# Second image of the first pair in chunks of 484 pixels, from rings of slots, in a polynomial convolution and attention kernel

## The chip, the cores and the metric

The kernel runs on one core of one Trainium2 chip. The metric is the device time of one execution in microseconds (us). A core has five engines with an instruction queue each: TensorE (PE, matmuls into PSUM), VectorE (DVE), ScalarE (ACT), GpSimd (POOL) and SyncE (SP). Transfers (DMAs) between HBM and SBUF are issued by instructions in the queues of SP and ACT. Instructions of one queue run in order; engines wait for each other through semaphores.

## The reference

The input x is 32 images of 64 channels and 56 x 56 = 3136 pixels, in float32. Two layers follow each other.

```
# layer 0, per group of 8 channels (8 groups), per pixel
p2 = x[:, :, _I2] * x[:, :, _J2]                 # 36 products of two
y2 = einsum('bgihw,goi->bgohw', p2, W2) + b2
p3 = x[:, :, _I3] * x[:, :, _J3] * x[:, :, _K3]  # 120 products of three
y3 = einsum('bgihw,goi->bgohw', p3, W3) + b3
l = inp + y2 * beta2 + y3 * beta3 * CONV3_SCALE
# layer 1, per image
g = clip(bn(conv1x1(l, w_inside)), 0, 6)
theta = l[:, :32]
f = einsum('niab,nicd->nabcd', theta, theta)     # 3136 x 3136 scores
f = softmax(f over the first pixel index)
f = softmax(f over the second pixel index)
out = einsum('nabcd,nicd->niab', f, g) / h * w
out = bn(depthwise_conv3x3(out)) + l
```

The scores are symmetric, so the first softmax of a column is that of a row, and both are done on a tile of 128 rows and 3136 columns.

## The kernel before, in words

The 32 images are worked on as 16 pairs (n = 0 to 15). The two images of a pair share the 128 partitions. Per pair there are IT = 49 tiles of attention: 24 of 128 pixels for each image and one that holds the last 64 pixels of both.

A tile t runs as follows. `scores` (twice, the two halves of the 3136 columns) multiplies theta by theta on PE into PSUM tile ps, and DVE turns the sign and keeps the minimum (tile e, first and second half; nm is the running minimum). `first_softmax` and `second_softmax` are two exponentials on ACT over 128 x 3136. Three tiles later `attend` multiplies e by g on PE into the accumulators av and the front of ax. So a tile has two half-steps, each with a `scores`, half an `attend`, and one place ("aux0", "aux1") for a unit of other work on PE.

The units are the polynomial of layer 0 and the 1x1 convolution g, both into the back of the same PSUM bank, ax. The polynomial of an image pair is cut in chunks of PCH = 242 pixels (NPC = 13, list PCS, line 37). Per chunk and per k (k counts the four groups of 32 partitions of outputs; ALL is the four of a pair, TWO the two of the second image alone) five rotated copies of x are loaded (names 0, a, 2, 4, b; b comes as two DMAs of 64 partitions), and for the whole chunk one pair c. POOL multiplies: q = x0 * xa, then four products p of q with 0, 2, 4 and b, and one product of the pair c. PE then multiplies six rounds (q, four p, the c product) by weights into ax (`poly`, line 452), and DVE adds bias and x and writes y (`poly_out`, line 469). A unit of the first pair's second image has three rounds, a unit of a whole pair two.

The order of all queues is written out in Python: `Pinned` (line 100) chains the instructions of an engine in the order of the calls. The loop at line 889 goes tile by tile. It calls `advance`, which drives the generators `products` (POOL's multiplications) and `prefetch`, which starts loads in the order of `plan` while there is room (`held` against `XB`, line 315: 7 slots for x0, 13 for the other copies, 3 for c) and credit (up to 8 transfers for a half-step in the first pair). `ROOM` (line 359) is the same for products: 8 slots for q, 20 for the others.

The first image of pair 0 goes another way (lines 222 to 297 and 747 to 797): seven chunks of FW = 448 pixels, loads in turn by SP's and ACT's queues (`first_loads`), products on DVE (`first_products`), polynomial into PSUM banks of their own (`first_poly`), output by DVE (`first_out`), then g (`first_g`). The batch norms of layer 1 (lines 285 to 302) stand after the products of chunk 1 and before the output of chunk 0; they need two square roots on ACT (`rsqrt_eps`). At chunk 5 `load_theta` starts for the first 2240 pixels, and the loads of the second image are fed with a credit of 12. After the last output `load_theta` loads the other 896 pixels, as four DMAs on SP's queue.

The second image of pair 0 (TWO, 13 chunks, 26 units) and the whole of pair 1 (ALL, 13 chunks, 39 units), with nine g units each, are then spread over the 98 half-steps of pair 0. Later pairs have one pair's units in theirs.

What the change touches: the batch norms, `load_next` (326), `prefetch` (354), `products` (362), `poly` (452), `poly_out` (469), `load_theta` (483), `poly_unit` (720), the loop at 780 and `rounds` (809).

Of the kernel before, what the change touches and what calls it, by code (L numbers as in the profile page):

```python
# [9 lines left out]
FP = mybir.dt.float32  # L10
AF = mybir.ActivationFunctionType
ALU = mybir.AluOpType
# [4 lines left out]
C = G * CPG  # L17
CRED = C // 2
H = W = 56
N = H * W  # L20
# [13 lines left out]
AUX = (NBL - NK * PER) * CG  # L34
NPC = -(-N // (BANK - AUX))
PCH = -(-N // NPC)
PCS = [(p, min(PCH, N - p)) for p in range(0, N, PCH)]
NROT = 6
EXT = CPG + NROT - 1
GM = 3  # L40
# [16 lines left out]
NRND = 5  # L57
# [12 lines left out]
def tile_poly_conv_attention(  # L70
# [61 lines left out]
    at = 0  # L132
# [40 lines left out]
    def col(name):  # L173
        return colt[:, COLS.index(name) : COLS.index(name) + 1]

    def row(name):
        return rowt[:, ROWS.index(name), :]
# [27 lines left out]
        return [t[:, p : p + FW] for t in tiles for p, _ in FCS]  # L205

    fx, fp = parts(firsts), parts(ys[1:] + [tt])
    fat = {"x": 0, "p": 0, "q": 0}
    fxs = {}
    frs = {}  # L210

# [70 lines left out]
    first_loads(2)  # L282


    s1 = rsqrt_eps("bn1", row("var1"), C)
    dve.tensor_tensor(s1, s1, row("gamma1"), ALU.mult)
    for j in range(2):
        dve.tensor_tensor(wit[:, j, :], wit[:, j, :], s1, ALU.mult)
    bias1 = const.tile([128, C], FP, name="bias1")
    dve.tensor_tensor(bias1, row("mean1"), s1, ALU.mult)  # L290
    dve.tensor_tensor(bias1, row("beta1"), bias1, ALU.subtract)
    bias1r = const.tile([128, GM, C], FP, name="bias1r")
    for k in range(GM):
        dve.tensor_copy(bias1r[:, k, :], bias1)


    s2 = rsqrt_eps("bn2", col("var2"), 1)
    dve.tensor_tensor(s2, s2, col("gamma2"), ALU.mult)
    dve.tensor_scalar(wdt, wdt, s2, W / H, ALU.mult, ALU.mult)
    bias2 = const.tile([128, 1], FP, name="bias2")  # L300
    dve.tensor_tensor(bias2, col("mean2"), s2, ALU.mult)
    dve.tensor_tensor(bias2, col("beta2"), bias2, ALU.subtract)

    prods = {}
    NB = 5
    BLK = [(b * H // NB, (b + 1) * H // NB) for b in range(NB)]
# [2 lines left out]

    XB = {"x0": 7, "xs": 13, "xc": 3}
    held = dict.fromkeys(XB, 0)
    plan = []
    loaded = {}
    PACE = 4.5
    credit = [1e9]  # L320

    def start(out, in_):
        credit[0] -= 1
        sync.dma_start(out=out, in_=in_)

    def load_next():
        tag, key = plan.pop(0)
        n, c, ks, name, k = key
        p0, w = PCS[c]
        held[tag] += 1  # L330
        ident = f"{n}_{c}_{ks[0]}_{k}"
        if name == "c":
            t = xp.tile([128, 2, PCH], FP, name=f"xc_{ident}", tag=tag, bufs=XB[tag])
            at = slice(ks[0] * 32, ks[-1] * 32 + 32)
            for d in range(2):
                src = bass.AP(
                    x.tensor,
                    ((4 * n + ks[0]) * EXT + 4 * d) * 4 * N + p0,
                    [[EXT * 4 * N, len(ks)], [N, 32], [1, w]],
                )  # L340
                start(t[at, d, :w], src)
            loaded[key] = [t[at, d, :w] for d in range(2)]
            return
        t = xp.tile([128, PCH], FP, name=f"x{name}_{ident}", tag=tag, bufs=XB[tag])
        for s0, every, d, grow in LOADS[name]:
            src = bass.AP(
                x.tensor,
                ((4 * n + k) * EXT + d) * 4 * N + p0,
                [[N, 32], [grow * 4 * N, NSLOT // every], [1, w]],
            )  # L350
            start(t[s0::every, :w] if every > 1 else t[:, :w], src)
        loaded[key] = t[:, :w]

    def prefetch():
        while plan and held[plan[0][0]] < XB[plan[0][0]] and credit[0] >= 1:
            load_next()


    ROOM = {"q": 8, "pr": 20}
    taken = dict.fromkeys(ROOM, 0)  # L360

    def products(n, c, ks):

        p0, w = PCS[c]
        ident = f"{n}_{c}_{ks[0]}"

        def use(name, k=None):  # L370
            key = n, c, ks, name, k
            return loaded.pop(key)

        x0 = {}
        rounds = [{}]
        both = []
        prods[n, c, ks] = rounds, both
        yield "q", len(ks)
        for k in ks:
            yield "load", (n, c, ks, "a", k)  # L380
            x0[k] = use("0", k)
            xa = use("a", k)
            q = prp.tile([128, PCH], FP, name=f"q_{ident}_{k}", tag="q", bufs=ROOM["q"])[:, :w]
            pool.tensor_tensor(q, x0[k], xa, ALU.mult)
            rounds[0][k] = q
            held["xs"] -= 1
            prefetch()
        for r, of in enumerate(("0", "2", "4", "b")):
            rounds.append({})
            yield "pr", len(ks)  # L390
            for k in ks:
                if of != "0":
                    yield "load", (n, c, ks, of, k)
                xr = x0[k] if of == "0" else use(of, k)
                p = prp.tile([128, PCH], FP, name=f"p_{ident}_{k}_{r}", tag="pr", bufs=ROOM["pr"])[:, :w]
                pool.tensor_tensor(p, rounds[0][k], xr, ALU.mult)
                rounds[-1][k] = p
                held["x0" if of == "0" else "xs"] -= 1
                prefetch()
        at = slice(ks[0] * 32, ks[-1] * 32 + 32)  # L400
        yield "load", (n, c, ks, "c", None)
        yield "pr", 1
        both += use("c")
        p4 = prp.tile([128, PCH], FP, name=f"p4_{ident}", tag="pr", bufs=ROOM["pr"])[at, :w]
        pool.tensor_tensor(p4, both[0], both[1], ALU.mult)
        rounds.append({k: p4 for k in ks})

# [41 lines left out]
                ax[:, AUX : AUX + GM * C].rearrange("p (q c) -> p q c", c=C), bias1r  # L449
            )  # L450

    def poly(n, c, ks, rs):

        p0, w = PCS[c]
        rounds = prods[n, c, ks][0]
        at = slice(ks[0] * 32, ks[-1] * 32 + 32)
        for r in rs:
            for k in ks:
                pe.matmul(
                    out=ax[k * 32 : k * 32 + 32, AUX : AUX + w],  # L460
                    lhsT=wq[:, r, k % 2, :] if r < NRND else w4[at, k * 32 : k * 32 + 32],
                    rhs=rounds[r][k],
                    start=False,
                    stop=(r == NRND),
                    skip_group_check=True,
                )
            taken["pr" if r else "q"] -= 1 if r == NRND else len(ks)

    def poly_out(n, c, ks):

        p0, w = PCS[c]
        at = slice(ks[0] * 32, ks[-1] * 32 + 32)
        assert n < 3 or all((n - 3, b) in stored for b in range(NB))
        xc = prods.pop((n, c, ks))[1][0]
        held["xc"] -= 1
        dve.scalar_tensor_tensor(
            ys[n % 3][at, p0 : p0 + w], ax[at, AUX : AUX + w], bias0[at], xc, ALU.add, ALU.add
        )


    ths = {}

    def load_theta(b, c0=0, c1=N):
        y = ys[b // 2 % 3]
        p0 = (b % 2) * C
        if c0 == 0:
            ths[b] = thp.tile([128, N], FP, name=f"th_{b}", tag=f"th{b % 2}")
        for r in range(4):
            start(ths[b][r * 32 : r * 32 + 32, c0:c1], y[p0 : p0 + CRED, c0:c1])

    def g_in(n, qs, j):

# [191 lines left out]
            f()  # L684

    LAG = 3
    ALL, ONE, TWO = (0, 1, 2, 3), (0, 1), (2, 3)
    last = NP * IT


# [26 lines left out]

            put(hs // 2, f"aux{hs % 2}", go)

    def poly_unit(n, c, ks, rs, hs):  # L720
        ends = rs[-1] == NRND
        unit(
            hs,
            FOR_POLY,
            lambda: poly(n, c, ks, rs),
            (lambda: poly_out(n, c, ks)) if ends else None,
            1 + 3.6 * len(rs),
        )
        if ends and c == NPC - 1:
            for j in (0, 1):  # L730
                if 2 * j in ks:

                    t = hs // 2 + 1 if j == 0 or n == 0 else (n * IT) + 2
                    put(t, "loads", lambda j=j: load_theta(2 * n + j))
# [39 lines left out]
                g_out(0, qs, 0)  # L774
                prepare(FOR_G if qs[0] < NQ else FOR_POLY)

    prepare(FOR_G)
    NF = len(FCS)
    first_poly(0)
    for c in range(1, NF):  # L780
        first_poly(c)
        first_out(c - 1)
        if c + 2 < NF:
            first_loads(c + 2)
        if c + 1 < NF:
            first_products(c + 1)
        if c == 5:
            load_theta(0, 0, FCS[5][0])

            for b in range(NPC):  # L790
                feed(0, b, TWO)
            credit[0] = 12
            advance()
        first_g(c - 1)
    first_out(NF - 1)
    load_theta(0, FCS[5][0], N)
    first_g(NF - 1)


# [4 lines left out]
    for n in range(NP):  # L804
# [2 lines left out]
        ga = [("g", n + 1, qs, 0) for qs in GS]  # L807

        def rounds(m, c, ks, per):
            return [("p", m, c, ks, list(range(r, r + per))) for r in range(0, NRND + 1, per)]  # L810

        todo = []
        if n == 0:
            for c in range(NPC):
                todo += rounds(0, c, TWO, 3)
            todo += gb
            for c in range(NPC):
# [188 lines left out]
```

## Time and profile before

| what | value |
|---|---|
| median of 3 runs | 4962.83 us (4959.59 to 4973.32) |
| the profiled execution, its own time | 4963.24 us |
| span of the profiled execution | 4961.4 us |
| busy share PE, ACT, DVE, POOL | 95%, 92%, 83%, 65% |
| mean granted TensorE clock | 0.988 |
| chain that ended last, by engine | PE 76%, DVE 12%, DMA 3%, issue 3%, ACT 3%, POOL 1%, SPq 1% |

How to read it. A busy row has the busy time of an engine, its share of the span and the instructions. In the slices each digit is tenths of a slice of 124 us. All recorded instructions carry line 108 (the helper), so groups are told apart by tiles: `first` and `first_s` are buffers of the first image, x, xa, xb and xc the loads of later chunks, q and p their products, ps the scores, e the softmax tile, th theta. A row of the timeline has start, length, engine, operation, output and inputs with shape, how many follow each other, and in brackets the idle time before it with what ended it. SPq and ACTq are DMA issues of SP's and ACT's queue.

### The profile page before, as it was taken

The page shows a single profiled execution, that of the slowest core. Times are in us where ns is not written, and L with a number is a line of the kernel's source. Part 1 is how long each engine was busy: PE and PEld are TensorE (multiplying, and loading weights), DVE is VectorE, ACT ScalarE, POOL GpSimd, SP SyncE. Part 2 cuts the span into 40 slices and gives each one's busy share as a digit, 9 for nine tenths or more (in the row PEclk, how much of TensorE's full clock was granted, in tenths as well). Part 3 has the DMA queues.
Part 4 walks back from the last instruction along what each step waited for, and adds up shares of the span by engine and source line. Part 5 has one row for each costly group of instructions (what it writes and reads, how often), then busy time and mean ns, then how long its engine had stood idle before and what let it go on. Part 6 is the DMA issues. An engine that isn't in the chain of part 4 may idle for free.

```text
span 4961.4 us, 263901 instructions
## 1 busy us (share of the span) xinstructions
PE 4711.5 (95%) x118068; PEld 3211.9 (65%) x118068; DVE 4136.2 (83%) x6106; ACT 4554.6 (92%) x2356; POOL 3212.2 (65%) x4325
## 2 busy tenths in 40 slices
PE   6988999999999999999999999999999999999885
PEld 2555666666666666666666666666666666666663
DVE  6545898988888898898988888888888888888787
ACT  1767999999999999999999999999999999999995
POOL 2676685857758586785857678585876858587000
PEclk9999999999999999999999999999999999999997
DMA  7555656565565556556565555656555565654101
GB/s 203 148 154 150 147 143 154 144 149 143 146 148 147 139 150 149 139 143 150 146 146 148 147 142 144 145 152 145 144 150 144 145 145 146 153 142 117 39 8 33
DMA packets 884029, 685.64 MB, mean 138 GB/s; under 512 B 290892, under 2 KB 868428, under 8 KB 878796
## 3 DMA queue, kind: packets, MB, share of 16 engines
q1 hardware_dynamic: 874892, 659.46, 52.1%
q8 instruction: 923, 15.12, 1.3%
q10 hardware_dynamic: 8000, 9.30, 0.6%
q14 instruction: 214, 1.75, 0.1%
HBM read 565.65 MB, written 25.69 MB: 119 GB/s over the span
## 4 chain that ended last, share of the span: by engine, by line
PE 76%; DVE 12%; DMA 3%; issue 3%; ACT 3%; POOL 1%; SPq 1%; ACTq 0%; POOLq 0%; DVEq 0%
PE av L108 33%; PE ps L108 25%; PE ax L108 18%; DVE e L108 10%; ACT e L108 3%; DMA xc_None<-in_x_dram 2%; DVE y L108 1%; SPq L108 1%; POOL p L108 1%; DVE num L108 1%; DMA x<-in_x_dram 1%; DMA first<-in_x_dram 1%; POOL q L108 0%; DMA xa<-in_x_dram 0%; ACTq L108 0%
## 5 line engine op out<-in xcount | busy, mean ns | idle before, releaser
L108 PEld LDWEIGHTS av<-gq,e 128*64 128x64 f32 x64512 | 2015.8, 138 | 945.6 <-issue 938.6
L108 ACT ACTIVATE e<-e,nm 128x3136 f32<-128x3136 f32 x784 | 2283.6, 2913 | 279.9 <-DVE e L108 264.0
L108 POOL TENSOR_TENSOR p<-q,x 128x242 f32<-128x242 f32 (+1 forms) x2418 | 1820.2, 786 | 842.6 <-PE ax L108 834.8
L108 ACT ACTIVATE e<-e,rz 128x3136 f32<-128x3136 f32 x784 | 2270.5, 2896 | 0.0
L108 PE MATMUL av<-gq,e 128*64 128x65 f32 x64512 | 2229.3, 225 | 4.3 <-ACT e L108 3.0
L108 DVE TENSOR_SCALAR_CACHE_REDUCE e<-ps 128x1568 f32<-128x1568 f32 x784 | 1403.4, 1790 | 312.7 <-PE ps L108 295.4
L108 DVE TENSOR_SCALAR_CACHE_REDUCE e<-ps,nm 128x1568 f32<-128x1568 f32 x784 | 1448.3, 1847 | 256.9 <-PE ps L108 251.4
L108 PE MATMUL ps<-th 32*64 32x392 f32 x25088 | 1450.2, 515 | 120.6 <-DVE e L108 110.8
L108 DVE SCALAR_TENSOR_TENSOR y<-tt,wdt,y 128x605 f32<-128x605 f32 (+4 forms) x720 | 726.2, 1009 | 6.7 <-DMA tt<-tr 5.2
L108 POOL TENSOR_TENSOR p<-q,xb 128x242 f32<-128x242 f32 x806 | 574.9, 740 | 218.8 <-PE ax L108 208.5
L108 POOL TENSOR_TENSOR q<-x,xa 128x242 f32<-128x242 f32 x806 | 570.9, 732 | 204.9 <-DMA xa<-in_x_dram 195.5
L108 PEld LDWEIGHTS ps<-th 32*64 32x64 f32 x25088 | 369.9, 130 | 463.1 <-DVE e L108 381.6
L108 PE MATMUL ax<-gq,e 128*64 128x65 f32 x12288 | 490.3, 222 | 1.2 <-issue 1.2
L108 PE MATMUL ax<-p,wq 128*32 128x242 f32 (+1 forms) x6448 | 477.8, 374 | 2.4 <-POOL p L108 1.4
L108 PEld LDWEIGHTS ax<-gq,e 128*64 128x64 f32 x12288 | 425.4, 138 | 1.5 <-issue 1.5
L108 PEld LDWEIGHTS ax<-p,wq 128*32 128x32 f32 x6448 | 178.4, 109 | 108.4 <-POOL p L108 15.7
L108 POOL TENSOR_SCALAR y<-y,bias 128x616 f32<-128x616 f32 (+1 forms) x80 | 149.1, 1864 | 149.2 <-PE ax L108 149.2
L108 DVE SCALAR_TENSOR_TENSOR y<-ax,bias,xc_None 128x242 f32<-128x242 f32 (+3 forms) x208 | 97.1, 467 | 120.7 <-PE ax L108 115.1
L108 POOL TENSOR_TENSOR p<-xc_None 128x242 f32<-128x242 f32 (+3 forms) x208 | 127.6, 614 | 105.2 <-DMA xc_None<-in_x_dram 85.3
L108 PE MATMUL ax<-p,w 128*32 128x242 f32 (+1 forms) x1612 | 125.1, 373 | 33.2 <-POOL p L108 33.2
L108 PE MATMUL ax<-wit,y 128*64 128x64 f32 x3136 | 143.8, 223 | 10.2 <-issue 6.1
L108 ACT ACTIVATION_READ_ACCUMULATOR e<-e,nm 128x1 f32 x784 | 145.7, 186 | 0.0
(80 smaller groups left out, 1348.9 us busy)
## 6 DMA issues: line engine op xcount, KB each, us to landing
x<-in_x_dram SPq DMA_DIRECT2D x2232, 121.0 KB
xa<-in_x_dram SPq DMA_DIRECT2D x744, 121.0 KB
xb<-in_x_dram SPq DMA_DIRECT2D x1488, 60.5 KB
th<-y SPq DMA_DIRECT2D x124, 392.0 KB
xc_None<-in_x_dram SPq DMA_DIRECT2D x360, 121.0 KB
x<-in_x_dram SPq DMA_DIRECT2D x186, 116.0 KB
out_dram<-y SPq DMA_DIRECT2D x64, 308.0 KB
tt<-tr SPq DMA_DIRECT2D x128, 100.0 KB
```

What stands on the lines that cost most here:

```text
L108: i = f(*args, **kw)
```

## The change

Chunks of the second image of pair 0 become 484 pixels wide for loads and for products (six of 484 and one of 232); matmuls and outputs stay at 242 wide, as two parts (sub) of a chunk, each with its two units. Where the slots for x0, the other copies, c, q and the products were buffers of a pool, each kind is now one tile used as a ring; a wide load or product takes two neighbouring slots. The rings for loads have 6 and 14 slots. The c pair of a wide chunk takes the whole c ring. Room is given back when the last part of a chunk has been used.

The batch norms move into the loop, after the products of chunk 2. The loop calls the g of chunk 5 after the output of chunk 6 and after the second part of theta, which goes by ACT's queue.

```diff
+DCS = [(p, min(2 * PCH, N - p)) for p in range(0, N, 2 * PCH)]
...
-    XB = {"x0": 7, "xs": 13, "xc": 3}
+    XB = {"x0": 6, "xs": 14, "xc": 3}
...
-    def start(out, in_):
+    def start(out, in_, queue=sync):
         credit[0] -= 1
-        sync.dma_start(out=out, in_=in_)
+        queue.dma_start(out=out, in_=in_)
+
+    ring = {t: [xp.tile([128, m, PCH], FP, name=f"ring_{t}", tag=t, bufs=1), 0] for t, m in XB.items() if t != "xc"}
+    ringc = xp.tile([128, 2 * XB["xc"] * PCH], FP, name="ring_xc", tag="xc", bufs=1)
+
+    def chunks(ks):
+        return DCS if len(ks) < len(ALL) else PCS
+
+    def many(w):
+        return -(-w // PCH)
+
+    def take_ring(tag, w):
+        t, at = ring[tag]
+        m, size = many(w), t.shape[1]
+        if at % m or at + m > size:
+            at = 0
+        ring[tag][1] = (at + m) % size
+        return t[:, at : at + m, :].rearrange("p m w -> p (m w)")[:, :w]
...
-        held[tag] += 1
+        held[tag] += XB["xc"] if name == "c" and many(w) > 1 else many(w)
...
     def prefetch():
-        while plan and held[plan[0][0]] < XB[plan[0][0]] and credit[0] >= 1:
+        while plan and credit[0] >= 1:
+            tag, (_, c, ks, _, _) = plan[0]
+            m = many(chunks(ks)[c][1])
+            if held[tag] + (XB[tag] if tag == "xc" and m > 1 else m) > XB[tag]:
+                return
             load_next()
...
-                    rhs=rounds[r][k],
+                    rhs=rounds[r][k][:, px],
...
-            taken["pr" if r else "q"] -= 1 if r == NRND else len(ks)
+            if ends:
+                taken["pr" if r else "q"] -= (sub + 1) * (1 if r == NRND else len(ks))
...
-        xc = prods.pop((n, c, ks))[1][0]
-        held["xc"] -= 1
+        xc = prods[n, c, ks][1][0][:, px]
+        if ends:
+            del prods[n, c, ks]
+            held["xc"] -= XB["xc"] if sub else 1
...
-    prepare(FOR_G)
     NF = len(FCS)
     first_poly(0)
     for c in range(1, NF):
...
         if c + 1 < NF:
             first_products(c + 1)
+        if c == 1:
+
+            s1 = rsqrt_eps("bn1", row("var1"), C)
...
+            prepare(FOR_G)
         if c == 5:
             load_theta(0, 0, FCS[5][0])
 
-            for b in range(NPC):
+            for b in range(len(DCS)):
                 feed(0, b, TWO)
             credit[0] = 12
             advance()
-        first_g(c - 1)
+        if c + 1 < NF:
+            first_g(c - 1)
     first_out(NF - 1)
-    load_theta(0, FCS[5][0], N)
+    load_theta(0, FCS[5][0], N, act)
+    first_g(NF - 2)
     first_g(NF - 1)
...
         def rounds(m, c, ks, per):
-            return [("p", m, c, ks, list(range(r, r + per))) for r in range(0, NRND + 1, per)]
+            return [
+                ("p", m, c, ks, list(range(r, r + per)), sub)
+                for sub in range(many(chunks(ks)[c][1]))
+                for r in range(0, NRND + 1, per)
+            ]
```

The batch norms are the same instructions as before, moved as a whole (`rsqrt_eps` with var1 and var2, the scaling of wit and wdt, bias1, bias1r and bias2).

## The prediction

> **What bounds the kernel now.** I read the page first (shares, the span in 40 slices), then the table of busy time by stage, the groups of PE by stage, and the timeline of the first 250 us.
>
> ```profile
> PE   6988999999999999999999999999999999999885
> ACT  1767999999999999999999999999999999999995
> POOL 2676685857758586785857678585876858587000
> ```
>
> From the fifth slice on ACT is at nine tenths and PE at nine: the steady pattern, which this change hardly touches. Slices 1 to 4 (to 496 us) are the first image, and then the first pair with twice the polynomial work beside its attention. Only that part can move. Columns of the next view: the stretch, its length, then busy us and instructions of PE, PEld, DVE, ACT, POOL, then PE clock, DMA share, GB/s.
>
> ```profile
> 36.00:40.00 4.00, 0.21 (x2) 0.00 (x0) 3.13 (x16) 0.46 (x2) 0.00 (x0) 0.99 0.09 25
> 40.00:44.00 4.00, 1.74 (x15) 1.26 (x17) 3.79 (x14) 0.00 (x0) 0.00 (x0) 0.50 0.75 216
> 120.00:215.00 95.00, 83.23 (x1590) 50.02 (x1584) 45.42 (x71) 61.01 (x33) 70.96 (x109) 0.96 0.53 141
> 265.00:465.00 200.00, 173.76 (x3672) 106.36 (x3666) 100.71 (x158) 133.63 (x70) 149.32 (x227) 0.93 0.55 148
> 1000.00:1290.00 290.00, 284.47 (x7324) 196.88 (x7316) 252.39 (x371) 281.13 (x146) 203.66 (x275) 1.00 0.57 144
> ```
>
> 120 to 215 us is the second image of the first pair. PE is idle in only 11.8 of its 95 us, so that is nearly all that any change of loads or products can win there. 265 to 465 us is pair 1's products; there all 26 loads of a chunk are of the old size after the change too. At 36 us the transfers stop for 4 us; that belongs to the batch norms.
>
> ```profile
> 157.70 0.61 POOL L108 TENSOR_TENSOR p<-xc_None 64x242 f32<-64x242 f32 x1 [1.94 <-DMA xc_None<-in_x_dram]
> 158.37 0.60 PE L108 MATMUL ax<-p,w 64*32 64x242 f32 x4 [0.94 <-POOL p L108]
> 160.86 1.11 SPq L108 DMA_DIRECT2D xc_None<-in_x_dram  x2
> ```
>
> This is the stall of that stage: POOL waits for the last load of the chunk (xc), PE for the product of it. SP is the reason that xc is late: a chunk has 14 issues, each about 0.6 us with what lies between (this xc pair: 1.11), 8.7 us of a period of 9.63 (y is written at 118.36 and, ten chunks later, at 214.69).
>
> **The change, part by part.**
>
> *Batch norms later.* Before, DVE stood from 31.6 to 36.3 us for ACT's square root, which stood behind eight DMA issues, and the work itself took until 41.6.
>
> ```profile
> 36.30 0.55 DVE L108 RECIPROCAL r_bn<-s_bn 128x64 f32<-128x64 f32 x1 [4.64 <-ACT s_bn L108]
> 39.44 32.48 ACTq L108 DMA_DIRECT2D first<-in_x_dram  x32
> ```
>
> After, the first thing DVE does is the output of chunk 0, which waits for PE's polynomial of chunk 1; PE ended that at 36.2 in the old trace. So the same 4.7 us are waited for another reason. Then output (0.65) and products of chunk 2 (42.08 to 47.97, so 5.9) end at about 42.8. Now the batch norms: ACT first has eight more issues (chunk 3's), which earlier ran at 22.25/24 = 0.93 us each, from 34.7 to some 42.5 or, held by the eighth transfer before, 43.3; then the table load (1.28) and the root (0.26): 45. DVE waits 2.2 and works 5.2 (36.30 to 41.59): to 50.2. In the listing of the two programs PE's 59,036 instructions stand in the same order, and there the g matmuls of chunk 0, which need the batch norm's weights and the bias in ax, stand ahead of the polynomial of chunk 2. So PE idles from 36.2 to 50.2. Earlier, chunk 2's polynomial ran beside its products; now it comes after them alone: 0.9 for g, then 4.83 at full clock (31.38 to 36.21), and about 6.8 at the granted 0.50 of the row above. DVE's queue holds the output of chunk 1 behind it, and chunk 3's products behind that. These start at 50.44 before and at about 58.6 after: **+8.1 us**, at best (full clock, no wait for ACT) +4, at worst +9. Given back: loads ran ahead meanwhile, so DVE's later wait of 2.87 us for a transfer (at 69.0) goes. The first image ends **+5.2 us** later (range +1 to +6).
>
> *Theta's last part by ACT's queue, and the output of the last chunk ahead of two g groups.* Before:
>
> ```profile
> 90.32 2.49 SPq L108 DMA_DIRECT2D th<-y  x4
> 91.68 4.39 PE L108 MATMUL ps<-th 32*64 32x392 f32 x16 [1.96 <-DVE e L108]
> 98.02 2.91 ACT L108 ACTIVATE e<-e,nm 128x3136 f32<-128x3136 f32 x1 [24.11 <-DVE e L108]
> ```
>
> The second half of the first scores took 4.39 us where the next one like it takes 1.61: **-2.8 us** for the first softmax. But it costs elsewhere. Each transfer waits on the eighth before it (eight semaphores in turn, over both queues), and in the changed program the fourth, fifth, seventh and eighth load of image 2 have theta's four ACT transfers as theirs. They cannot leave before theta has landed, some 3 us after the last output (83.1 + 5.2). Before, SP issued twelve loads ahead of theta. So xa's second load leaves at about 92 and lands at 97, nine products follow.
>
> *Chunks of 484 pixels.* Seven chunks in place of 13: 98 issues in place of 182, and 66 POOL products fewer. A 484-wide product: the rows have 705 ns at 242 and 682 at 232, so between 1.26 us (that slope) and 1.41 (twice); I take 1.33, near both. Ten products and the xc one (0.61 at 242, so 1.15): 14.5 us of POOL per double chunk. SP needs 14 x 0.62 = 8.7 us for twice the pixels: it no longer paces. The Trainium skill ("GPSIMD Engine Reference", Elementwise) has 4497 ns for 2048 elements, which as an estimate would be 1.06 us; the rows here are dearer, and by either POOL stays under PE. The skill's page "DMA: Bandwidth & Descriptors" (Specifications) speaks against a gain from the size itself: line rate from 512 B, and the old rows had 968 B. The trace agrees as far as it goes, since the engines were at 0.53; the gain counted here is that of issues, not of bytes.
>
> What is late next is xc: it now fills its whole ring, so the next xc transfer waits for the output of the second half of the chunk before. From that output to the next chunk's first output: output 0.5 and semaphore 0.1, two issues 1.1, landing 4.4 to 5.1 (rows from the end of an xc issue to POOL's start: 103.00 to 107.39, 308.93 to 314.05), product 1.15, matmul and semaphore 0.7: 8.0 to 8.7 us. PE has two half-steps of other work in that time, 7.8 us (169.13 to 177.77 less 0.84 idle). The stall is 0.2 to 0.9 per double chunk, in place of 2 x 1.2. PE's own work is 83.23 us in 95, so 16.9 per 19.26: a cycle of **17.1 us** for 19.26 (16.4 at full clock and no stall; 18 with both at their bad ends).
>
> *Rings of 6, 14 in place of 7, 13.* In the 265 to 465 us stretch SP issues without a pause (18.4 us for 26), so slots don't pace it, and pair 1 has 224 separate SP waits for 219: nothing, within +1 and, if a slot less waited for did shorten each of 13 chunks by one POOL product's 0.55 us, -7. The steady part has POOL waiting for PE (78 us in 300), which hides all of it.
>
> **The sum.** First image +5.2. First double chunk: its xc product ends at about 110.4 (97.2 + nine products 12.0 + 1.15); PE closes the first half at 111 and the second two half-steps of 3 us later, at 117.0 for 110.57: +6.4. The next output is POOL's (110.4 + 14.5 + 0.7 = 125.6 for 118.36): +7.2. Then five cycles: 5 x (17.1 - 19.26) = -10.8. Net **-3.6 us** at the end of image 2 (214.7). What follows, the g units (39.3 us, PE bound, with pair 1's first product ready 18 us early) and the 18.5 us cycles set by SP, shifts as a whole. The profiled execution is 4963.24 (span 4961.4 and 1.8 around it), 0.4 from the median of the runs: 4963.2 - 3.6 = 4959.6, so **4959 us**.
>
> **Rivals.**
>
> 1. *Faster:* the first image loses only the +1 of its good end, xc is hidden, and the cycle is PE's own 16.4: +3 at the second double chunk, then 5 x -2.9: -11.5. If the extra slot also helps pair 1 (-7): 4945. For it: clock 0.96 and 0.93 in the stalled stages against 1.00 in steady state, so fewer stalls also give a faster PE. Against: PE's order forces the late polynomial of chunk 2. Chance 0.23.
>
> 2. *Slower:* xc, one slot and one transfer behind the output. If its landing takes over 6.9 us, as it could behind four 242 KB loads, the cycle passes 19.3 and image 2 costs more than before. At 8.2 us it is 20.6: 5 x 1.3 = +6.7, with the late start (+7.2, and 2 for a clock that falls at each long stall, as ps at 1.61 for 0.92 after the stall at 296 us): about 4979. Against it: the transfers ahead of xc are issued long before. Chance 0.14.
>
> 3. *No effect at all:* SP's queue paces pair 1 from its first chunk, and what image 2 wins is waited for there: 4963 + 0 to 3. Against: pair 1's first xc product ended at 233, PE needed it at about 250. Chance 0.1; it lies within 0.3%, as my forecast does (0.53).
>
> **How the numbers follow.** 0.3% is 15 us, about what a measurement of this kernel can tell from no change. Faster by more: rival 1 with the slots' help and a little beyond, 0.23. Slower by more: 0.14. The rest, 0.63. The range goes from rival 1 to rival 2: 4943 to 4979.
>
> **What would show it.** DVE idle for ACT's root at about 43, then for PE until about 58, and products of chunk 3 at 58 (not 50). The first exponential at about 100.5. Outputs of image 2 in pairs, 17 us apart, the 13th at about 211; POOL's wait before the xc product short, PE's before it under 1 us. If the outputs are 19 us apart, xc is the wait; if chunk 3's products start by 52, my order of PE is not what counts. A steady cycle of pair 1 other than 18.5 would make the forecast wrong in the part that I put at nothing.

## The result, and the profile after

The changed kernel took **4984.76 us** (median of 4 runs, 4981.95 to 4985.69) beside 4963.57 for the kernel before in the same session: ratio 1.0038, 95% interval 1.0023 to 1.0053. The interval straddles 0.3%; the sign is clear. It is slower by 21 us, where 4959 was forecast. The profiled execution has a span of 4980.2 us (before 4961.4).

The same stages as before, from the table of busy time by stage of the changed kernel (columns as there: stretch, length, busy us and count of PE, PEld, DVE, ACT, POOL, then PE clock, DMA share, GB/s):

```profile
36.00:40.00 4.00, 0.88 (x5) 0.07 (x4) 3.08 (x6) 0.00 (x0) 0.00 (x0) 1.00 0.89 270
40.00:44.00 4.00, 0.00 (x0) 0.00 (x0) 3.68 (x9) 1.54 (x2) 0.00 (x0) 0.54 0.90 282
120.00:215.00 95.00, 77.48 (x1389) 46.46 (x1386) 39.23 (x62) 52.82 (x28) 54.95 (x47) 0.87 0.43 122
265.00:465.00 200.00, 180.65 (x3874) 110.55 (x3868) 106.55 (x167) 139.91 (x73) 151.09 (x227) 0.97 0.57 149
1000.00:1290.00 290.00, 284.48 (x7302) 196.12 (x7297) 252.52 (x370) 281.18 (x147) 204.24 (x275) 1.00 0.57 145
```

The transfers no longer stop at 36 us, and the steady stage is what it was. In 120 to 215, the stage of image 2, PE had 1389 matmul records for 1590, its clock fell from 0.96 to 0.87, and the DMA engines were less busy, not more. So a wait has grown there. The outputs of image 2 (y in DVE's timeline) tell how it adds up: the second half of the first double chunk at 118.20, the sixth's at 229.69, so a cycle (the two outputs of a double chunk) of 111.49/5 = **22.3 us** for 19.26 before; the last output at 236.97 for 214.69, **+22.3**; the last output of pair 1 at 485.28 for 465.38, +19.9. Behind that about this shift is carried to the end (+18.8 in the span).

One cycle of the changed kernel, its timeline from the output that frees xc's ring:

```profile
140.91 0.47 DVE L110 SCALAR_TENSOR_TENSOR y<-ax,bias,ring_xc 64x242 f32<-64x242 f32 x1 [1.14 <-PE ax L110]
141.41 1.11 SPq L110 DMA_DIRECT2D ring_xc<-in_x_dram  x2
151.55 1.23 POOL L110 TENSOR_TENSOR ring_pr<-ring_xc 64x484 f32<-64x484 f32 x1 [6.64 <-DMA ring_xs<-in_x_dram]
152.83 0.96 PE L110 MATMUL ax<-ring_pr,w 64*32 64x242 f32 x4 [4.77 <-POOL ring_pr L110]
153.83 0.48 DVE L110 SCALAR_TENSOR_TENSOR y<-ax,bias,ring_xc 64x242 f32<-64x242 f32 x1 [6.33 <-PE ax L110]
```

From output to output 12.9 us: semaphore and issues 1.6, then 9.0 from the end of the issue to POOL's start, product and matmul 2.3. The bracket of the third row names ring_xs, but that product reads only ring_xc; other rows of the kind name ring_xc. SP's queue shows the same from another side: the eighth transfer after each of the two, which waits for it, leaves at 147.47 and at 151.45, so the two landed one after the other, the second just before the product. Over the six 484-wide rows the landing, from the end of the issue to the product's start, was 7.2 to 9.6 us, where the two old rows of the prediction had 4.4 and 5.1.

At the end of one such wait, when the other loads have all but ended, the table by stage shows what is left:

```profile
218.00:218.40 0.40, 0.00 (x0) 0.00 (x0) 0.00 (x0) 0.32 (x1) 0.00 (x0) 1.00 0.19 51
```

A share of 0.19 is about three of the 16 DMA engines, with what may be left of other loads among them, and 51 GB/s is a third of the 141 that the stage moved before. At that end xc is late while most engines have nothing to do. Earlier in the wait it is otherwise (three stretches of the cycle above):

```profile
142.50:144.00 1.50, 1.50 (x34) 1.11 (x32) 1.11 (x2) 1.50 (x3) 1.50 (x3) 1.00 0.13 32
148.00:149.00 1.00, 0.06 (x2) 0.00 (x0) 0.00 (x0) 1.00 (x1) 0.00 (x0) 1.00 1.09 303
149.00:150.00 1.00, 0.00 (x0) 0.00 (x0) 0.00 (x0) 1.00 (x1) 0.00 (x0) 1.00 0.98 242
```

At first xc is almost alone, with a share of 0.13, about two engines. Then the loads issued behind it keep all 16 busy until past 150 us, xc's engines among them.

**Theory T**, formed from these rows: a transfer of xc, 64 partitions with the two images as its slowest dimension, is carried by very few DMA engines, and being one slot behind the output it stands whole in the chain. **Rivals**: R1, it is late only because it queues among the 242 KB loads issued around it; R2, only SP's order matters, not the landing; R3, the start-up part of the change costs the time; R4, the partitions of a transfer count, not the engines.

### The profile page after: what moved, and what is told of

Same layout as the page of the kernel before. It is cut to its first block, busy times and chain, and to the rows that moved or that the text cites. A ratio compares the mean times of both kernels' runs of the same rounds, so it can differ in the third digit from the quotient of the medians.

```text
span 4980.2 us, 263825 instructions
## 1 busy us (share of the span) xinstructions
PE 4714.0 (95%) x118068; PEld 3210.4 (64%) x118068; DVE 4133.2 (83%) x6106; ACT 4553.8 (91%) x2356; POOL 3204.9 (64%) x4259
## 4 chain that ended last, share of the span: by engine, by line
PE 77%; DVE 12%; DMA 3%; issue 3%; ACT 3%; POOL 1%; SPq 1%; ACTq 0%; POOLq 0%; DVEq 0%
PE av L110 33%; PE ps L110 25%; PE ax L110 18%; DVE e L110 10%; ACT e L110 3%; DMA ring_xc<-in_x_dram 2%; DMA ring_xs<-in_x_dram 1%; POOL ring_pr L110 1%; DVE y L110 1%; SPq L110 1%; DVE num L110 1%; PE first L110 0%; PE first_s L110 0%; DMA first<-in_x_dram 0%; DMA th<-y 0%
## 5 line engine op out<-in xcount | busy, mean ns | idle before, releaser
L110 POOL TENSOR_TENSOR ring_pr<-ring_q,ring_xs 128x242 f32<-128x242 f32 (+2 forms) x2382 | 1783.9, 783 | 555.0 <-PE ax L110 522.7
L110 POOL TENSOR_TENSOR ring_pr<-ring_q,ring_x 128x242 f32<-128x242 f32 (+2 forms) x794 | 606.4, 789 | 582.7 <-PE ax L110 579.0
L110 POOL TENSOR_TENSOR ring_q<-ring_x,ring_xs 128x242 f32<-128x242 f32 (+2 forms) x794 | 568.8, 743 | 163.9 <-DMA ring_xs<-in_x_dram 160.3
L110 PE MATMUL ax<-ring_pr,wq 128*32 128x242 f32 (+1 forms) x6448 | 478.6, 373 | 4.1 <-POOL ring_pr L110 2.7
L110 PEld LDWEIGHTS ax<-ring_pr,wq 128*32 128x32 f32 x6448 | 178.1, 109 | 112.7 <-POOL ring_pr L110 18.8
L110 DVE SCALAR_TENSOR_TENSOR y<-ax,bias,ring_xc 128x242 f32<-128x242 f32 (+3 forms) x208 | 97.1, 467 | 133.5 <-PE ax L110 127.6
L110 POOL TENSOR_TENSOR ring_pr<-ring_xc 128x242 f32<-128x242 f32 (+2 forms) x202 | 128.1, 634 | 97.1 <-DMA ring_xc<-in_x_dram 74.0
L110 PE MATMUL ax<-ring_pr,w 128*32 128x242 f32 (+1 forms) x1612 | 126.2, 373 | 43.3 <-POOL ring_pr L110 43.3
## 6 DMA issues: line engine op xcount, KB each, us to landing
ring_xs<-in_x_dram SPq DMA_DIRECT2D x1440, 60.5 KB
```

Source lines behind the costliest of these rows:

```text
L110: i = f(*args, **kw)
```

## The experiments

Each was timed beside the kernel before on its own chip; the ratios are to that.

**xc by image.** The edit (only chunks of image 2):

```diff
-            for d in range(2):
...
-                    ((4 * n + ks[0]) * EXT + 4 * d) * 4 * N + p0,
-                    [[EXT * 4 * N, len(ks)], [N, 32], [1, w]],
...
-                start(t[at, d, :w], src)
+            for i in range(2):
...
+                        x.tensor, (4 * n + ks[i]) * EXT * 4 * N + p0, [[N, 32], [16 * N, 2], [1, w]]
...
+                    start(t[ks[i] * 32 : ks[i] * 32 + 32, :, :w], src)
```

> The changed kernel with xc's two transfers split the other way: one for each image (32 partitions with both polynomial terms) in place of one for each term (64 partitions, images in the slowest dimension). The same number of transfers and of bytes, the same slot, the same waits. Theory T (the two halves of a wide xc land some 9 us after their issue because a transfer with the two images as its slowest dimension is carried by few of the 16 DMA engines): landing falls to 3 to 5 us, the cycle of a double chunk of image 2 from 22.3 to about 17 us, so 5 x -5.2 = -26 and some 4 more at the first double chunk: 4954 to 4961 us. Rival R1 (xc lands late because it queues among the 242 KB loads issued around it): landing and cycle stay, 4982 to 4988 us. Rival R3 (the loss is the start-up's): the same, 4982 to 4988. The Trainium skill, page 'DMA: Bandwidth & Descriptors', section 'Why a DMA increments its semaphore by 16 and not by 1', lets the slowest dimensions decide over how many engines a transfer is spread; by it these would be 2 engines as the change has it and 16 here.

Measured: 4946.83 us, ratio 0.9964 (0.9951 to 0.9976). R1 and R3 would have left the time as it was. So the loads can delay xc only through the few engines that it has and shares with them. The stage, and two steps of the chain, in this kernel:

```profile
120.00:215.00 95.00, 94.52 (x2030) 59.14 (x2024) 59.66 (x96) 75.39 (x40) 71.34 (x74) 1.00 0.52 150
```

```profile
161.45 0.79 SPq L110 DMA_DIRECT2D ring_xc<-in_x_dram  x2
165.15 1.23 POOL L110 TENSOR_TENSOR ring_pr<-ring_xc 64x484 f32<-64x484 f32 x1
192.38 0.80 SPq L110 DMA_DIRECT2D ring_xc<-in_x_dram  x2
194.81 0.59 POOL L110 TENSOR_TENSOR ring_pr<-ring_xc 64x232 f32<-64x232 f32 x1 [3.98 <-DMA ring_xc<-in_x_dram]
```

The same bytes, in the same number of transfers, behind the same output, amid the same loads: at 165.15 POOL did not wait at all (so landing under 2.9 us), and the narrow last one landed in 1.6. PE is busy in 94.5 of 95 us, and the outputs are 7.72 us apart: a cycle of 15.4, under the 17 that I expected. One distance is longer, 10.1 us, with PE busy too; over the same five cycles as above the mean is 15.9. The shorter cycle is part of why the time lies below theory T's forecast, here and in the next run.

**Two slots.** A wide pair takes two of four slots; the transfers are as in the change.

```diff
-    XB = {"x0": 6, "xs": 14, "xc": 3}
+    XB = {"x0": 6, "xs": 14, "xc": 4}
...
-        held[tag] += XB["xc"] if name == "c" and many(w) > 1 else many(w)
+        held[tag] += many(w)
...
-            o = 0 if many(w) > 1 else fat["c"] % XB["xc"] * 2 * PCH
-            fat["c"] += many(w) == 1
+            o = fat["c"] % XB["xc"] * 2 * PCH
+            fat["c"] += many(w)
```

> The changed kernel with two wide slots for xc in place of one, so that the xc transfers of a double chunk no longer wait for the last output of the one before. The transfers themselves are as in the changed kernel. Theory T and rival R1 both put the loss on a landing of 9 us that stands in the chain from one output to the next; with a slot more the landing lies beside other work: cycle 17 to 18 us, 4954 to 4964 us, with landings of 8 to 9 us as before. Rival R2 (the landing does not matter, only that xc is one of fourteen loads in SP's order): cycle stays at 20 to 22, 4975 to 4988. Rival R3 (start-up): 4982 to 4988.

Measured: 4942.66, ratio 0.9957 (0.9945 to 0.997). R2 falls: SP's order and the transfers' form are those of the change.

```profile
110.56 1.10 SPq L110 DMA_DIRECT2D ring_xc<-in_x_dram  x2
120.87 1.22 POOL L110 TENSOR_TENSOR ring_pr<-ring_xc 64x484 f32<-64x484 f32 x1
```

xc is now issued before the output at 116.10, and the product follows 9.2 us after the issues without waiting. The landing lies beside other work; the outputs were 7.7 us apart again. Both halves of T are needed for the loss: few engines, and the one slot.

**The start-up.** Three runs: the batch norms alone put back (the block under `if c == 1` at its old place, and `prepare(FOR_G)` ahead of the loop); the whole start-up as before, so that the chunks and rings are left alone; and the start-up part alone on the kernel before. Apart from the block that moves, the second differs from the change by

```diff
-        if c + 1 < NF:
-            first_g(c - 1)
+        first_g(c - 1)
     first_out(NF - 1)
-    load_theta(0, FCS[5][0], N, act)
-    first_g(NF - 2)
+    load_theta(0, FCS[5][0], N)
```

> The changed kernel with the batch norms back in their old place, all else as in the changed kernel (theta's last part by ScalarE's queue too). Theory T: products of chunk 3 start at about 50.5 us again in place of 57.5, the first scores some 4 us earlier, but the nine loads of image 2 that wait for theta move with it; the cycle of image 2 stays at 22.3: 4979 to 4984 us. Rival R3 (the loss comes from the start-up): 4960 to 4966 us.

Measured: 4981.85, ratio 1.0032 (1.002 to 1.0045), as theory T has it.

> Only the chunks of 484 pixels and the rings; batch norms, theta's queue and the order of the g matmuls as before the change. Theory T: the start of image 2 is that of the kernel before, within 3 us (first double chunk's second output near 112 in place of 118.2), the cycle stays at 22.3 us: 4976 to 4982 us. Rival R3: 4958 to 4966 us. What this run leaves above the kernel before is the price of the chunks alone; what it leaves below the changed kernel is that of the start-up part.

Measured: 4979.07, ratio 1.0029 (1.0019 to 1.0039), cycle (222.07 - 110.26)/5 = 22.4 us. Some 13 of the 21 us are there without the start-up part (4979.07 beside 4965.66), and the cycle is that of the change: R3 falls as the main cause. The start-up adds the rest, which the timelines show at image 2's beginning: xc's first pair leaves at 91.80 here and at 97.90 in the change, behind the nine loads that wait for theta, and the first double chunk's second output comes at 110.26 here and at 118.20 there.

> The kernel before with the start-up part of the change alone: batch norms later, theta's last part by ScalarE's queue, the last output ahead of two g groups. Chunks, rings and xc as before. The changed kernel less the one with the chunks alone was 5.7 us, so if the parts add up: 4968 to 4973 us beside 4965.7 for before. The prediction's terms (+5.2 for the first image, -2.8 for theta, +7.2 at image 2's second chunk) would give 4968 to 4973 too. If the first image's delay is given back by SP, which has run ahead meanwhile, nothing: 4962 to 4967.

Measured: 4966.21, ratio 1.0004 (0.9995 to 1.0013). Here I missed: the start-up alone costs nothing that can be told. So it costs only beside wide chunks whose xc lands late; with a fast xc it again costs nothing that shows (last runs below).

**The old chunks with xc by image.** The same edit of the loads on the kernel before.

> The kernel before (chunks of 242, old start-up) with its xc transfers of image 2 split by image in place of by term, nothing else. Theory T (the layout of xc's transfers sets how long they take, in the old size too: 4.4 us from the end of the issue to POOL's start at 2 x 60.5 KB): landing near 2 us, the waits of POOL (1.94) and PE (0.94) for it go, and SP's 8.7 us of issues per chunk are the floor under 9.63: some 11 chunks x -0.9 = -10, so 4952 to 4959 us beside 4965.7 for before in the last runs. Rival A (what the run with xc by image gained over before, 19 us, is the layout's alone and the wider chunks give nothing): 4943 to 4950 us. Rival B (xc is not on the path at the old size): 4962 to 4968 us.

Measured: 4968.04, ratio 1.001 (1.0002 to 1.0019). This one contradicted theory T's forecast. Half of it held: xc landed early.

```profile
121.77 1.01 SPq L108 DMA_DIRECT2D xc_None<-in_x_dram  x2
122.83 0.54 SPq L108 DMA_DIRECT2D x<-in_x_dram  x1
123.47 0.55 SPq L108 DMA_DIRECT2D xa<-in_x_dram  x1
124.06 0.60 SPq L108 DMA_DIRECT2D x<-in_x_dram  x1
124.44 0.61 POOL L108 TENSOR_TENSOR p<-xc_None 64x242 f32<-64x242 f32 x1 [0.26 <-DMA xc_None<-in_x_dram]
124.76 0.55 SPq L108 DMA_DIRECT2D xa<-in_x_dram  x1
125.40 3.62 SPq L108 DMA_DIRECT2D x<-in_x_dram  x4
129.12 2.48 SPq L108 DMA_DIRECT2D xb<-in_x_dram  x4
131.69 1.01 SPq L108 DMA_DIRECT2D xc_None<-in_x_dram  x2
```

It took 1.7 us (122.78 to 124.44). But the next xc leaves 9.92 us after this one: 14 issues with the waits among them pace the old chunks, and the floor of 8.7 that I used lacks these waits (3.62 for four issues, which elsewhere take 2.48). By the view of waits, from 120 to 215 us SP waited 15.0 us for POOL to free slots, and POOL 18.5 us for xa: the two queues hold each other up. So the gain of the run by image is not the layout's alone: with the old chunks the layout wins nothing, with the wide chunks and the old layout time is lost, and only both together win.

**Four narrow transfers.** Each wide xc transfer cut in two by pixels, the images still slowest.

```diff
+                for o1 in range(0, w, PCH):
+                    w1 = min(PCH, w - o1)
...
-                    [[EXT * 4 * N, len(ks)], [N, 32], [1, w]],
+                        [[EXT * 4 * N, len(ks)], [N, 32], [1, w1]],
...
-                start(t[at, d, :w], src)
+                    start(t[at, d, o1 : o1 + w1], src)
```

> The changed kernel with each wide xc transfer of image 2 cut in two by pixels: four transfers of 64 partitions x 242, images still in the slowest dimension, so in the form that the kernel before had. One slot, as in the change. If a transfer of this form has few engines for itself, but each transfer other ones (theory T with engines taken in turn): 4 x 60.5 KB lie side by side, landing 4.5 to 6 us, cycle 17 to 19, 4955 to 4968 us. If all transfers of this form go over the same few engines (theory T with fixed engines), or if xc only queues with the loads around it (R1): landing 8 to 10 us as in the change, plus 1.1 us for two more issues: 4984 to 4994 us.

Measured: 4966.75, ratio 1.0002 (0.9994 to 1.0011). It falls between, and does not tell what it was made for: in SP's timeline the first of the four leaves soon after the first half's output (108.56; issue at 109.98), the other three only after the second's (115.47; issues from 115.98). Cutting by pixels let that first one wait for the first output alone, which I had not seen.

**31 and 1, 30 and 2.** The kernel by image, each transfer cut once more, by partitions. The two sisters differ in one number, 31 here and 30 there:

```diff
+                    for s0, s1 in ((0, 31), (31, 32)):
...
+                            [[N, s1 - s0], [16 * N, 2], [1, w]],
...
+                        start(t[ks[i] * 32 + s0 : ks[i] * 32 + s1, :, :w], src)
```

> The kernel with xc by image (one wide slot), each of its two wide transfers cut in two: 31 partitions and 1. Against its sister run (30 and 2) the number of transfers, the bytes, the waits and the loads around are the same; only the divisors of the partition count differ (31 has none). Theory T in its sharp form (the number of DMA engines of a transfer follows from a divisor of its slowest dimension): two transfers of 120 KB on one engine each, and on the same one: slower than in the change, where the tail of a transfer showed 0.19 of 16 engines and 51 GB/s, so about 25 GB/s each: 240 KB on one engine are some 9.5 us, landing 10 to 12, cycle 24 to 26: 4988 to 5010 us. Rival R4 (what helped in the run by image was the smaller number of partitions of a transfer, or that the terms of a partition travel together): as there, landing 2 to 4 us, 4946 to 4958 us. The Trainium skill, page 'DMA: Bandwidth & Descriptors', section 'Why a DMA increments its semaphore by 16 and not by 1', states that divisor rule, and that the lowest-numbered engines are taken.

> As the run with 31 and 1, but cut into 30 partitions and 2 (30 has the divisor 15). Theory T: landing 2 to 4 us, cycle 15.5 to 17 us; two issues more per double chunk (1.2 us of SP, not on the path): 4946 to 4958 us. If cutting itself costs (four transfers, or small ones of 1 or 2 partitions): both sisters alike, 4965 us or more.

Measured: **5010.35** (ratio 1.009, 1.0076 to 1.0104) with 31 and 1, **4948.73** (0.9967, 0.9955 to 0.9979) with 30 and 2. Sixty microseconds for one partition; the run with 31 lies 0.35 us past T's forecast, the one with 30 within it. With 31 (timeline, then the table by stage at the end of that wait):

```profile
148.07 2.21 SPq L110 DMA_DIRECT2D ring_xc<-in_x_dram  x4
161.64 1.21 POOL L110 TENSOR_TENSOR ring_pr<-ring_xc 64x484 f32<-64x484 f32 x1 [10.06 <-DMA ring_xc<-in_x_dram]
```

```profile
159.50:161.50 2.00, 0.00 (x0) 0.00 (x0) 0.00 (x0) 0.41 (x1) 0.00 (x0) 0.50 0.07 22
```

With 30:

```profile
142.56 1.32 SPq L110 DMA_DIRECT2D ring_xc<-in_x_dram  x4
146.46 1.22 POOL L110 TENSOR_TENSOR ring_pr<-ring_xc 64x484 f32<-64x484 f32 x1
```

A DMA share of 0.07 is one engine of 16 (0.0625), moving 22 GB/s, while PE, DVE and POOL stand still for two microseconds. With 30 POOL does not wait here (at most 0.35 us in the six wide rows). R4 falls, since the partitions are almost the same in both. T's sharp form, that the divisors of the slowest dimension decide, forecast both sisters; the counts tried are these two, and the 2 and 32 of the change and the run by image.

**Both, and the best version.** xc by image with two slots on the changed kernel; the same with the batch norms back; the same with the whole start-up as before (edits as above).

> The changed kernel with both: xc's transfers split by image and two wide slots. In each of the two alone, image 2 ran at a cycle of 15.4 us with PE busy in 94.5 of 95 us, so nothing is left to win there (theory T: PE is the floor): outputs of image 2 stay 7.7 us apart. The run with two slots was 4 us shorter than the one with xc by image; if that came from the fourth slot of the ring in pair 1, both together give what two slots gave: 4938 to 4945 us. If xc's landing was still somewhere on the path with two slots: 4930 to 4937 us. If the gain of 4 us was the spread of runs: 4943 to 4948.

Measured: 4939.34, ratio 0.9954 (0.994 to 0.9968).

> Chunks and rings, xc by image, two wide slots, theta by ScalarE's queue, but batch norms in their old place. Beside the run with both (4939.3 us), which has the batch norms later. Where xc set the pace the old place was worth 2.9 us (4981.85 for 4984.76). If the first image's end is on the path now that image 2 no longer waits: 4934 to 4938 us. If it is given back by the loads that run ahead: 4937 to 4942 us.

Measured: 4937.35, ratio 0.9944 (0.9932 to 0.9957).

> Chunks and rings, xc by image and two wide slots, with the whole start-up as before the change (batch norms, theta's queue, order of the g matmuls). The candidate for the best version if the start-up part of the change costs: 4933 to 4938 us (the chunks alone were 5.7 us below the whole change). If theta by ScalarE's queue is worth its 2.8 us and nothing stands against it: 4938 to 4943 us.

Measured: 4938.5, ratio 0.9948 (0.9935 to 0.996). The three can't be told apart, so the place of the batch norms and theta's queue still are worth nothing that shows. Each beats the kernel before by about 0.5%. In all three image 2's outputs are 7.7 us apart, as expected (one distance is 10.1, as in the run by image). What the fourth slot adds shows in pair 1: from its first output to its last 201.6 to 205.8 us in the four kernels that have it, 209.0 to 215.1 in before, the change and the runs by image with three (one profile each; no run tests the slot alone).

## Why the prediction was wrong

**The step that failed** is the landing of xc, "4.4 to 5.1 (rows from the end of an xc issue to POOL's start ...)", which gave the cycle of 17.1. It measured 7.2 to 9.6, and the cycle 22.3. The mechanism, one slot behind the output, was named rightly, and also as rival 2; the price was taken from rows that looked near but were not. These are the rows, of the kernel before:

```profile
101.90 1.10 SPq L108 DMA_DIRECT2D xc_None<-in_x_dram  x2
107.39 0.61 POOL L108 TENSOR_TENSOR p<-xc_None 64x242 f32<-64x242 f32 x1 [1.36 <-DMA xc_None<-in_x_dram]
307.77 1.16 SPq L108 DMA_DIRECT2D xc_None<-in_x_dram  x2
314.05 0.61 POOL L108 TENSOR_TENSOR p<-xc_None 128x242 f32<-128x242 f32 x1 [2.54 <-DMA xc_None<-in_x_dram]
```

Read by the divisor of the slowest dimension, as the sisters bear out, both of those rows moved 60.5 KB per engine: two transfers of 60.5 KB with 2 images slowest, or (the row from pair 1) two of 121 KB with 4. The wide one moves two of 121 KB with 2: twice as much per engine. At the 51 GB/s of the tail that is 2 x 121 x 1.024 / 51 = 4.9 us, an estimate, beside some 2.4 for the old size; so 4.4 becomes 6.8 at least.

The rest of the 9 us is probably the loads that share those engines. From 142.5 to 151.5 us the trace has 1.84 MB moved; less xc's 0.25, a sixteenth of the rest is 0.10 MB, so each of xc's two engines would have carried 0.12 + 0.10 MB in 9.0 us, 25 GB/s, beside 22 for the one busy engine of the run with 31 and 1. That is an estimate, which takes the loads as evenly spread; no run here separates it.

The reason given against rival 2, that the transfers ahead of xc leave long before, was true and did not help, since it is the loads behind xc that share its engines. Rival 2 gave 4979 at a landing of 8.2; it was 22.3 instead of 20.6 per cycle, and 21 us in all instead of 16. Part of that is the other half of the cycle, from a double chunk's first output to its second: 8.9 to 12.6 us, where the run by image has 7.7 (once 10.1). After the wait the matmuls of the scores are slower, 1.61 us at 153.72 for 0.91 before it.

The Trainium skill, page "DMA: Bandwidth & Descriptors", section "Why a DMA increments its semaphore by 16 and not by 1", has the rule: a transfer runs on the largest number of engines, at most 16, that divides the slowest dimension of both sides. That makes 2 for the change's xc, 16 for xc by image, 1 for 31 partitions and 15 for 30. The runs agree in order and sign (4984.76, 4946.83, 5010.35, 4948.73 us); the share of 0.07 is that of one engine, the 0.13 of the change that of two (0.125), and its 0.19 at the end of a wait lies somewhat above. The prediction weighed another section of this page, on the size of a row, which did not bear on the loss.

Point by point, as the prediction had them:

- *Batch norms later, +8.1 at chunk 3's products*: measured 50.44 to 57.49, +7.1, with DVE idle 5.88 for the polynomial. Its wait for ACT's root was 0.32, not 2.2. The sixth of the first image's seven outputs came at 86.22 for 82.38, +3.8 where +5.2 was forecast.

```profile
43.62 0.26 ACT L110 ACTIVATE s_bn<-v_bn 128x64 f32<-128x64 f32 x1 [1.44 <-DVE v_bn L110]
43.91 0.55 DVE L110 RECIPROCAL r_bn<-s_bn 128x64 f32<-128x64 f32 x1 [0.32 <-ACT s_bn L110]
56.88 0.68 DVE L110 SCALAR_TENSOR_TENSOR y<-first_s,bias,first 64x448 f32<-64x448 f32 x1 [5.88 <-PE first_s L110]
```

- *Theta by ACT, -2.8 for the first softmax; loads of image 2 held back*: right. Both halves of the scores took 1.61, the first exponential started at 98.71 (predicted 100.5, before 98.02), and SP's nine loads waited until 91.81. The cost of the start-up alone was put too high, since it is not measurable; beside the wide chunks it is in the +7.6 of the sum below.

```profile
87.73 2.56 ACTq L110 DMA_DIRECT2D th<-y  x4
91.81 6.05 SPq L110 DMA_DIRECT2D ring_xs<-in_x_dram  x9
95.09 1.61 PE L110 MATMUL ps<-th 32*64 32x392 f32 x16 [1.96 <-DVE e L110]
98.71 2.91 ACT L110 ACTIVATE e<-e,nm 128x3136 f32<-128x3136 f32 x1 [7.02 <-DVE e L110]
```

- *First double chunk's second output 117.0*: 118.20. *The next output 125.6*: 130.89, the first cycle with the late xc.
- *POOL's 484-wide product 1.33 us (1.26 to 1.41)*: 1.21 to 1.22, under the lower end. The means of 705 ns at 242 and 1215 at 484 make 2.1 ns per element and 0.2 us besides; the slope from 232 to 242 (2.3 ns) was too steep. POOL was not the bound, so it cost nothing.
- *SP no longer paces*: right for the wide chunks, whose outputs come 7.7 us apart in the run by image, where the old ones with a fast xc stay at 9.6 (mean of nine, from 118.96 to 205.48).
- *PE's floor 16.4*: 15.4 in the run by image. PE's busy time before holds slower matmuls: from 120 to 190 us the mean length of one matmul of the scores was 541 ns at a clock of 0.95 before, and 513 at 1.00 in the run by image.
- *Rings and pair 1, nothing*: right for the change; its cycle is 18.4 us for 18.6. The reason given, that slots don't pace SP there, does not hold: from 265 to 465 us SP waited 39.6 us for POOL before the change, and in the four runs with a fourth slot for xc pair 1 was shorter.
- *The sum*: five cycles of +3.0 in place of -2.2 (+15.2), and +7.6 at the first double chunk's second output (predicted +6.4): +22.8, measured +22.3 at image 2's last output.

## What to carry to other kernels

When a transfer grows or is regrouped, work out how many DMA engines carry it from its slowest dimension, and take the price of a row per engine, not per transfer; 64 partitions written as 2 x 32 were worth two engines here. Put the dimension with many divisors slowest: it cost no instruction, and turned a loss of 0.4% into a gain of 0.4%. A wide buffer that takes a whole ring puts its full landing into the chain from one use to the next; a second slot hid a landing of 9 us as well as a fast transfer removed it.

## What the runs showed of the hardware that was not expected

A single partition, 31 for 30 in the larger piece, moved the kernel by 62 us through one DMA engine at 22 GB/s. And a TensorE that stops waiting gains twice: in image 2's stage (120 to 190 us) its granted clock was 0.88 in the change, 0.95 before and 1.00 in the run by image, and the mean length of a matmul of the scores 601, 541 and 513 ns.
